# The first transfers of a recurrence-and-FFN kernel: x in four pieces, the gates' weights on another queue, one warming product less

## The chip, the cores and the metric

The kernel runs on one core of one Trainium2 chip. The metric is the device time of one execution in microseconds (us). The profile is one execution taken by the hardware profiler. Its engines are PE (TensorE: matrix products), PEld (TensorE's weight loads), DVE (VectorE), ACT (ScalarE), POOL (GpSimd) and SP (SyncE, which here issues nearly all transfers).

## The reference

The input x has 2 sequences of 4096 steps and 256 features. With sizes left out, the reference is

```python
u = x @ W_in + b_in                       # 64 states
g = sigmoid(x @ W_gate + b_gate)
h_t = tanh(h_{t-1} @ A + u_t @ Bm)         # along the 4096 steps
y_t = h_t @ C.T + u_t @ D.T
y_t = g_t * y_t + (1 - g_t) * x_t
x1  = layernorm(x + (y @ W_out + b_out + x))
ffn = gelu(x1 @ bin(w1).T + b1) @ bin(w2).T + b2   # bin(w) = mean|w| of a row times sign(w)
out = layernorm(x1 + ffn)
```

## The kernel before, in words

The recurrence is cut into segments: each sequence is split into 64 segments of 64 steps, so that one step handles 2 x 64 = 128 columns at once. The segments start from zero states 48 steps (`WARM`) ahead, and the kernel later checks that this warm-up was long enough. The steps are grouped into 16 chunks of 4 steps, with 512 columns each. One chunk's x in transposed form is a tile `xt` of 128 partitions x 2 x 512 numbers (512 KB); the middle index `k` is the half of the 256 features that lies on the partitions. The first chunk used is `FIRST` = 4, since the warm-up begins there; then come 5, 6 and so on.

The order of instructions on every engine is written out by hand, and each engine works its list in order. At the start TensorE's list is:

1. `idle_products`: products of a tile of ones with itself, which need no transfer (line 154).
2. `u_of_chunks(FIRST)`: u of chunk 4 (line 131). For each half `k` of the features there is one product for the first 256 columns (called LOW, written to the lower partitions of the result) and one for the other 256 (TOP). They need `wab` (W_in, A and Bm in one tile) and the tile `xt` of chunk 4. DVE and ACT add the bias and write u to `st` (lines 144 and 142).
3. `parts`: pieces of the gates' product of chunk 4 (line 313), which need `w_gate`, with a step of the recurrence (line 157; its tanh on ACT, line 158) put between each two.
4. `u_of_chunks(5, 6)`: u of chunks 5 and 6 together (line 131), where chunk 5 is LOW and chunk 6 is TOP. They need both tiles.
5. Further pieces of gates and steps, and u of the chunks 7 and 8, and so on. After the warm-up of the recurrence the later stages (mixing, projection, norms, the two layers of the FFN) are woven into the same list.

Each product of float32 numbers appears in the profile as two MATMUL passes.

The transfers at the start are issued by two engines, each with a queue of its own:

- ACT: `wab` (96 KB, line 109), `bias_c` (5.5 KB, line 111). After them comes its table load (line 120).
- SP: chunk 4 in two transfers of 256 KB, one for each `k` (line 104), `w_gate` (256 KB, line 112), then chunks 5, 6, 7, 8, 9, 10 and 11 whole (line 104), `cd`, `w_out`, and two rows of biases (lines 181 to 184).

A framework that builds the program gives each transfer one of eight completion semaphores in turn, and a transfer waits until the one that had the semaphore before it has landed. `x_tiles` has eight buffers (`XTB`), so later chunks also wait until a tile has been used.

Of the kernel before, what the change touches and what calls it, by code (L numbers as in the profile page):

```python
# [18 lines left out]
KD = DM // P  # L19
# [4 lines left out]
N = 512  # L24
# [13 lines left out]
def gated_recurrence_then_binary_ffn(  # L38
# [16 lines left out]
    nc = tc.nc  # L55
# [21 lines left out]
    w_gate = cp.tile([P, KD, DM], FP, name="w_gate")  # L77
# [20 lines left out]
    x_tiles = {}  # L98

    def load_xT(c, pieces=1):  # L100
        x_tiles[c] = xp.tile([P, KD, N], FP, tag="xt", name=f"xt{c}", bufs=XTB)
        for k in range(pieces):
            cut = slice(k * KD // pieces, (k + 1) * KD // pieces)
            nc.sync.dma_start(out=x_tiles[c][:, cut, :], in_=xT[c][:, cut, :])

    FIRST = (L - WARM) // SPC
    nc.gpsimd.memset(ones, 1.0)
    nc.gpsimd.memset(ab[:, S:], 0.0)
    nc.scalar.dma_start(out=wab[:, : KD * S + S], in_=W_in_AB)
    load_xT(FIRST, KD)  # L110
    nc.scalar.dma_start(out=bias_c, in_=biases)
    nc.sync.dma_start(out=w_gate, in_=W_gate)

    nc.gpsimd.memset(h_of[:, L - WARM, :, :], 0.0)
    nc.gpsimd.memset(h_of[:, 0, :, 0:1], 0.0)
# [8 lines left out]
    def u_of_chunks(*chunks):  # L124

        n = N * len(chunks) // 2
        parts = [(chunks[0], 0), (chunks[1], 0) if len(chunks) == 2 else (chunks[0], 1)]
        ps = p_1.tile([P, N], FP, tag="h", name=f"ps_u{chunks[0]}")
        for k in range(KD):
            for (c, i), r in zip(parts, (LOW, TOP)):  # L130
                nc.tensor.matmul(  # L131
                    ps[r, :n],
                    w_in[k],
                    x_tiles[c][:, k, bass.ts(i, n)],
                    start=k == 0,
                    stop=k == KD - 1,
                    skip_group_check=True,
                )
        for (c, i), r in zip(parts, (LOW, TOP)):
            to = u_of[:, bass.ds(c * SPC + i * n // W, n // W)].rearrange("p j b k -> p (j b k)")  # L140
            if r is TOP and c == FIRST:
                nc.scalar.activation(to, ps[r, :n], AF.Identity, bias=bin_c[r, :])
            else:
                nc.vector.tensor_scalar(to, ps[r, :n], bin_c[r, :], None, ALU.add)
        have_u.update(chunks)
        yield
# [4 lines left out]
    def idle_products(n):  # L151

        for _ in range(n):
            nc.tensor.matmul(p_h, ones, ones, start=True, stop=True)
# [174 lines left out]
    class Chunk:  # L329
# [10 lines left out]
        def load_gate_x(self):  # L340
            load_xT(self.c)
# [322 lines left out]
    def emit(what, pieces, pace=5600):  # L664
        nonlocal since
        for _ in pieces:
            since += COST.get(what, 0)
            if since >= pace:
                since = min(since - pace, pace // 2)
                if ready():  # L670
                    next_steps()
# [25 lines left out]
    with tc.manual_schedule(engines={ET.PE, ET.Activation, ET.DVE, ET.Pool, ET.SP}):  # L697
        waiting = []
        for c in range(FIRST + 1, FIRST + 6):
            load_xT(c)  # L700
        idle_products(7)
        emit("u", u_of_chunks(FIRST), 1 << 30)
        since = 0
        pairs = [(5, 6), (7, 8), (9, 10), (11, 12), (13, 14), (), (1, 2)]
# [224 lines left out]
```

## Time and profile before

| | before |
|---|---|
| median of 3 runs | 437.67 us (437.33 to 437.82) |
| time of the profiled execution | 437.67 us |
| its span, first to last instruction | 435.9 us |
| PE busy | 425.5 us, 98% of the span |
| DVE, ACT, POOL busy | 332.4, 286.0, 155.8 us |
| DMA moved | 51.34 MB, mean 118 GB/s |
| DMA in the first 5 of 40 slices | 297, 300, 282, 261, 269 GB/s |

All instants below are in us from the first instruction of the span. A profile line of a group gives line, engine, operation and tiles. In a timeline, the bracket at the end tells how long the engine was idle before the group and what ended it. "Busy" of PE means that a product was in its pipeline, not that it ran at its peak.

### The profile page before, as it was taken

To read this page: it belongs to the slowest core of one execution; us is meant where nothing else is said; L and a number is where in the kernel's file an instruction comes from. 1 tells how busy PE (TensorE), PEld (TensorE's weight loads), DVE (VectorE), ACT (ScalarE), POOL (GpSimd) and SP (SyncE) were. 2 spreads that over 40 slices of the span, in tenths; PEclk is the share of its full clock that TensorE was granted. 3 is DMA by queue.
4 is the path that set the end of the run, shared out by engine and by line. 5 is a ranking of instruction groups with operands and counts; after the bars stand their busy time and mean duration, and the time that the engine had idled before them with its cause. 6 is when DMAs were issued, how large, how long until landed. Compare 5 with 4: busy or idle time off the path is not lost.

```text
span 435.9 us, 6818 instructions
## 1 busy us (share of the span) xinstructions
PE 425.5 (98%) x2402; PEld 344.3 (79%) x2402; DVE 332.4 (76%) x569; ACT 286.0 (66%) x480; POOL 155.8 (36%) x176
## 2 busy tenths in 40 slices
PE   8999999999999999999999999999999999999992
PEld 5665767788888879797979797978888888888982
DVE  0245937895979798888888897979797979797674
ACT  2443452486587776767677776777767585849881
POOL 1000050474143435253525443444343444533413
PEclk9999999999999999999999999999999999999997
DMA  8877713400251615152426242534233232311102
GB/s 297 300 282 261 269 36 128 163 2 0 44 174 44 217 46 178 38 186 80 144 66 192 76 144 69 166 102 124 91 107 109 58 111 60 111 36 50 48 2 102
DMA packets 31479, 51.34 MB, mean 118 GB/s; under 512 B 5328, under 2 KB 19664, under 8 KB 31440
## 3 DMA queue, kind: packets, MB, share of 16 engines
q1 hardware_dynamic: 30864, 50.48, 36.4%
q8 instruction: 21, 0.34, 0.3%
q10 hardware_dynamic: 576, 0.37, 0.3%
q14 instruction: 18, 0.15, 0.1%
HBM read 31.43 MB, written 8.39 MB: 91 GB/s over the span
## 4 chain that ended last, share of the span: by engine, by line
PE 89%; DVE 5%; ACT 2%; DMA 1%; issue 1%; POOL 1%; SPq 0%; POOLq 0%; DVEq 0%
PE ps_h L486 25%; PE ps_o L528 25%; PE ps_g L313 12%; PE ps_z L399 11%; PE ps_y L374 6%; PE ps_s L157 6%; PE ps_u L131 3%; DMA xt<-in_xT 1%; DVE hlo L512 1%; ACT xn L278 1%; POOL rs_b L265 1%; PE ps_t L430 1%; DVE bs_b L255 1%; DVE d L381 1%; ACT h L496 1%
## 5 line engine op out<-in xcount | busy, mean ns | idle before, releaser
L528 PE MATMUL ps_o<-sg,hhi 128*128 128x256 f32 x496 | 121.4, 286 | 0.0
L528 PE MATMUL ps_o<-sg,hlo 128*128 128x256 f32 x496 | 117.9, 279 | 0.1
L496 ACT ACTIVATE h<-ps_h,bias_c,al 128x512 f32<-128x512 f32 x128 | 95.5, 771 | 16.8 <-PE ps_h L486 13.0
L528 PEld LDWEIGHTS ps_o<-sg,hhi 128*128 128x128 f32 x496 | 93.5, 189 | 1.1 <-DVE o L544 0.3
L528 PEld LDWEIGHTS ps_o<-sg,hlo 128*128 128x128 f32 x496 | 93.5, 188 | 1.1 <-DVE hlo L512 0.3
L486 PE MATMUL ps_h<-xhi,sg 128*128 128x512 f32 x256 | 92.9, 444 | 0.3 <-ACT h L496 0.3
L359 POOL TENSOR_TENSOR xn<-xn,bo_r 128x256 f32<-128x256 f32 x64 | 54.7, 888 | 88.6 <-DMA xn<-in_x 78.4
L512 DVE TENSOR_TENSOR hlo<-h,hhi 128x1024 fp32r<-128x1024 f32 (+1 forms) x65 | 79.5, 1240 | 5.0 <-ACT hhi L505 5.0
L486 PE MATMUL ps_h<-xlo,sg 128*128 128x512 f32 x256 | 80.1, 394 | 0.2
L265 POOL TENSOR_TENSOR rs_b<-rs_b,neg_half 128x4 f32<-128x4 f32 (+1 forms) x17 | 28.1, 1655 | 115.1 <-DVE rs_b L264 105.0
L505 ACT CAST hhi<-h 128x1024 fp32r<-128x1024 f32 (+1 forms) x65 | 67.4, 1039 | 2.0
L313 PE MATMUL ps_g<-xt,w_gate 128*128 128x384 f32 (+3 forms) x208 | 66.2, 430 | 0.1
L486 PEld LDWEIGHTS ps_h<-xhi,sg 128*128 128x128 f32 x256 | 46.5, 189 | 18.9 <-issue 11.7
L158 ACT ACTIVATE st<-ps_s 64x128 f32<-64x128 f32 x112 | 30.0, 268 | 45.7 <-PE ps_s L157 45.3
L486 PEld LDWEIGHTS ps_h<-xlo,sg 128*128 128x128 f32 x256 | 48.0, 188 | 11.9 <-DVE xlo L440 0.7
L157 PEld LDWEIGHTS ps_s<-st,wab 128*128 128x128 f32 x224 | 38.5, 189 | 21.6 <-ACT st L158 9.7
L359 POOL TENSOR_TENSOR xn<-xn,b_r 128x256 f32<-128x256 f32 x64 | 52.9, 855 | 1.1 <-PE ps_t L430 1.1
L399 PE MATMUL ps_z<-w_out,tg 128*128 128x256 f32 x224 | 50.6, 379 | 0.0
L399 PEld LDWEIGHTS ps_z<-w_out,tg 128*128 128x128 f32 x224 | 41.4, 190 | 5.1
L157 PE MATMUL ps_s<-st,wab 128*128 128x128 f32 x224 | 43.8, 277 | 0.1
L278 ACT ACTIVATE xn<-xn,nm_a,rs_a 128x256 f32<-128x256 f32 x60 | 31.2, 591 | 14.4 <-DVE nm_a L270 14.3
L265 POOL TENSOR_TENSOR rs_a<-rs_a,neg_half 128x4 f32<-128x4 f32 x16 | 17.2, 1072 | 65.0 <-DVE rs_a L264 63.0
(79 smaller groups left out, 481.5 us busy)
## 6 DMA issues: line engine op xcount, KB each, us to landing
xt<-in_xT SPq DMA_DIRECT2D x35, 512.0 KB, 4.4
xn<-in_x SPq DMA_DIRECT2D x16, 512.0 KB, 3.4
out_y<-xn SPq DMA_DIRECT2D x15, 512.0 KB, 2.6
xlo<-xb SPq DMA_DIRECT2D x208, 32.0 KB, 1.9
hu<-st SPq DMA_DIRECT2D x32, 128.0 KB, 2.3
w1t<-in_w1T SPq DMA_DIRECT2D x2, 512.0 KB, 4.9
w1n<-in_w SPq DMA_DIRECT2D x2, 512.0 KB, 6.1
w2t<-in_w2T SPq DMA_DIRECT2D x2, 512.0 KB, 5.2
```

The lines of the kernel that those rows point to most:

```text
L157: nc.tensor.matmul(p_h, ab, st[:, j].rearrange("p b k -> p (b k)"), start=True, stop=True)
L158: nc.scalar.activation(h_of[:, j + 1].rearrange("p b k -> p (b k)"), p_h[TOP, :], AF.Tanh)
L265: nc.gpsimd.tensor_tensor(rs, rs, neg_half[:, cut], ALU.pow)
L278: nc.scalar.activation(r, r, AF.Identity, bias=self.sh[:, i : i + 1], scale=rs)
L313: nc.tensor.matmul(ps[:, cut], w_gate[:, k, bass.ts(m, P)], xt_[:, k, cut], start=k == 0 and i == 0, stop=k == KD - 1, skip_group_check=True,)
L359: nc.gpsimd.tensor_tensor(r[:, i, :], r[:, i, :], row, ALU.add)
L399: nc.tensor.matmul(self.ps_z[:, i, :], self.y[:, k, bass.ts(i, P)], w_out[:, k, :], start=k == 0, stop=k == KD - 1,)
L486: nc.tensor.matmul(ps, sg1[:, k, bass.ts(j, P)], part[:, k, :], start=n == 0, stop=n == 2 * KD - 1,)
L496: nc.scalar.activation(to, ps.rearrange("p (a i c) -> p a i c", a=P // 32, c=32) if self.far else ps, AF.Gelu, bias=b1_c[:, j : j + 1], sc ...
L505: nc.scalar.copy(hi[:, part, :], h[:, part, :])
L512: nc.vector.tensor_sub(lo[:, i, :], h[:, i, :], hi[:, i, :].bitcast(FP))
L528: nc.tensor.matmul(ps[:, i, :], part[:, j % 2, bass.ts(tb, P)], sg2[:, j, :], start=j == 0 and part is self.h[j // 2][0] and first, stop=j ...
```

## The change

`load_xT` with `pieces=2` now cuts a chunk by half `k` and by half of the columns, so that the first chunk comes in four transfers of 128 KB, in the order in which its four products take them. A piece is 256 numbers, 1 KB, on each partition; before it was 512 numbers, 2 KB. `w_gate` is issued by ACT, between `wab` and `bias_c`, instead of by SP behind the first chunk. `idle_products` makes 6 products instead of 7. Nothing else in any engine's list changes its place; the semaphores of all later transfers move on by two.

```diff
     def load_xT(c, pieces=1):
         x_tiles[c] = xp.tile([P, KD, N], FP, tag="xt", name=f"xt{c}", bufs=XTB)
-        for k in range(pieces):
-            cut = slice(k * KD // pieces, (k + 1) * KD // pieces)
-            nc.sync.dma_start(out=x_tiles[c][:, cut, :], in_=xT[c][:, cut, :])
+        if pieces == 1:
+            nc.sync.dma_start(out=x_tiles[c], in_=xT[c])
+            return
+        for k in range(KD):
+            for i in range(pieces):
+                cut = bass.ts(i, N // pieces)
+                nc.sync.dma_start(out=x_tiles[c][:, k, cut], in_=xT[c][:, k, cut])
 
...
     nc.scalar.dma_start(out=wab[:, : KD * S + S], in_=W_in_AB)
-    load_xT(FIRST, KD)
+    load_xT(FIRST, 2)
+    nc.scalar.dma_start(out=w_gate, in_=W_gate)
     nc.scalar.dma_start(out=bias_c, in_=biases)
-    nc.sync.dma_start(out=w_gate, in_=W_gate)
...
-        idle_products(7)
+        idle_products(6)
         emit("u", u_of_chunks(FIRST), 1 << 30)
```

## The prediction

> **What bounds the kernel now.** I read the page first: shares, then the chain that ended last.
>
> ```profile
> PE 425.5 (98%) x2402; PEld 344.3 (79%) x2402; DVE 332.4 (76%) x569; ACT 286.0 (66%) x480; POOL 155.8 (36%) x176
> ...
> PE 89%; DVE 5%; ACT 2%; DMA 1%; issue 1%; POOL 1%; SPq 0%; POOLq 0%; DVEq 0%
> ```
>
> TensorE is busy nearly throughout and carries 89% of the chain. So a microsecond won or lost ahead of its unbroken stretch moves the end by about a microsecond, and one inside cover moves nothing. The edits lie in the first 9 us; which wait ends last there? The chain in order of time says it (start, duration, what):
>
> ```profile
> 2.14 0.43 SPq L104
> 2.57 0.04 issue
> 2.62 6.29 DMA xt<-in_xT
> 8.90 0.04 issue
> 8.94 1.93 PE ps_u L131 x6
> 10.87 0.42 PE ps_s L157 x2
> 11.29 0.66 PE ps_g L313 x4
> 11.95 0.22 PE ps_s L157 x2
> ```
>
> SP's issues run one behind the other, and the one begun at 2.62 lands at 8.90: it is the third tile, chunk 6 (the fifth entry on SP: two halves of chunk 4, `w_gate`, chunk 5, chunk 6). From 8.94 TensorE never stops: the windows 9 to 20, 20 to 40 and 40 to 60 us are 11.00, 20.00 and 20.00 us busy. **The landing of chunk 6 sets the time**, not the first x. TensorE's timeline shows how far ahead it was:
>
> ```profile
> 7.65 1.07 PE L131 MATMUL ps_u<-xt,wab 128*64 128x512 f32 x2
> 8.94 1.93 PE L131 MATMUL ps_u<-xt,wab 128*64 128x512 f32 x6 [0.22 <-DMA xt<-in_xT]
> ...
> 16.46 1.94 PE L131 MATMUL ps_u<-xt,wab 128*64 128x512 f32 x8
> ```
>
> Two of the eight passes for chunks 5 and 6 ran at 7.65 and the other six from 8.94. The next pair's eight take 1.94, no longer than those six, since the two halves run side by side. So the early two bought nothing: TensorE may reach this place as late as 8.94, **1.29 us later than it does**, at no cost.
>
> The waits of TensorE's weight loads up to 9.5 us (total, times, longest) are small before that:
>
> ```profile
> PEld ps_u L131 <- DMA xt<-in_xT: 1.6, 3, 1.1
> ...
> PEld ps_g L313 <- DMA w_gate<-in_W_gate: 0.6, 1, 0.6
> ...
> PEld ps_u L131 <- DMA wab<-in_W_in_AB: 0.3, 1, 0.3
> ```
>
> Only the 1.1 is chunk 6's. The rest, which the edits aim at, come before 7.65 and are inside the 1.29.
>
> Why does chunk 6 land at 8.90? The table by stretches (last columns: granted clock, DMA share, GB/s):
>
> ```profile
> 1.50:3.00 1.50, 1.50 (x9) 1.50 (x9) 0.00 (x0) 1.31 (x2) 0.29 (x1) 1.00 0.58 128
> 3.00:4.50 1.50, 1.50 (x9) 1.25 (x10) 0.00 (x0) 0.18 (x1) 0.00 (x0) 1.00 1.04 364
> 4.50:6.00 1.50, 1.38 (x9) 0.51 (x8) 0.64 (x2) 0.00 (x0) 0.00 (x0) 1.00 1.05 318
> 6.00:9.00 3.00, 2.75 (x14) 1.40 (x13) 0.02 (x1) 1.01 (x3) 0.00 (x0) 1.00 1.03 412
> ```
>
> From 3 us on the DMA engines are full. Landings, as issue plus "us to landing": first half of chunk 4 at 4.1, `wab` 4.3, second half 4.8, `bias_c` 5.0, `w_gate` 5.6, chunk 5 7.6, chunk 6 8.9, chunk 7 10.2. The last steps are 1.3 us for 512 KB, and 524 KB at 412 GB/s is 1.27: first in, first out at full rate. Chunk 6 is behind bytes, not behind its issue.
>
> **What the Trainium skill says.** "DMA: Bandwidth & Descriptors", section "Queues, rings and completion order": SP and ACT each own one row of rings on the same 16 engines, each ring consumed in order, the rows taken in turn by the packet. The trace agrees with order within SP's row (landings above). The same page, "Issuing engines are not separate DMA queues": a second issuing engine saves only issue time, here 0.43 us an issue. So `w_gate` on ACT's row shares the same rate. The same page, "Why small descriptors are slow (HBM only)": about 3 cycles for each packet beside one for each 32 bytes; 35 cycles for 1 KB against 67 for 2 KB is 4.5% more, an estimate. The trace's packet records have 84 ns for most 2 KB packets and 46 for most 1 KB ones, 9.5%; I take those. "TensorE: Matmul & The Clock Gate", Part 1: the clock doubles after some 3.4 us of sustained work. Here the warming passes begin at 1.01 and take 0.21 us each, against 0.11 for the same 128 columns at 11.95; the change comes at about 4.3.
>
> **The change, part by part.**
>
> *Four transfers for two.* SP issues four of 0.43 and loses `w_gate`'s: the pieces go at 0.76, 1.21, 1.67 and 2.14, chunk 5 at 2.62 instead of 2.14. Chunk 5's data wait for the ring anyway (5.5 us to landing, of which 1.3 is its own), so 0.48 is hidden; uncovered it would cost 0.48. The pieces' rows are 1 KB: 512 packets of 46 ns instead of 256 of 84, over 16 engines: 1.47 against 1.34, **+0.13 us** ahead of chunk 6, not hidden (0.06 by the skill's price).
>
> *Semaphores.* In the instruction list each DMA takes one of eight completion semaphores in turn, so the ninth waits for the first. Before, the first eight end with chunk 7, and chunk 8 waits for `wab`; SP's own waits show it:
>
> ```profile
> SPq L104 <- DMA wab<-in_W_in_AB: 0.8, 1, 0.8
> ```
>
> Now there are two more before, so **chunk 6 waits for `wab`**: issued at about 4.3 instead of 2.62. Queued behind it on SP are chunks 7 to 11, `cd`, `w_out`, the two rows; each waits for a DMA eight places ahead, long landed. Cover: first packets move 1.0 us after an issue (0.76 to 1.78), so chunk 6 is ready at about 5.3, while chunk 5 keeps the ring until about 7.1 (landing 7.6, some 0.5 after the last data by the packet records). 1.8 us of cover; cost 0. Chunks 7 and 8 aren't needed before 16.46.
>
> *`w_gate` on ACT.* Same bytes ahead of chunk 6; cost 0. It now shares with x, so it lands somewhat earlier than 5.6 and the last piece of x about when `w_gate` did, 5.5, instead of 4.8. The last products of chunk 4 take about 0.5: the gates begin at about 6.1 instead of 5.61, chunks 5 and 6 are reached at 8.15 instead of 7.65. Covered by the 1.29. ACT issues one more: `bias_c` goes at 1.65 and lands at 5.2 to 5.5, the table load ends at 3.4; ACT is first needed at 6.06, DVE's conversion moves by at most the same 0.5, and only the first steps wait for it, inside the same cover.
>
> *One product less.* Two passes, 0.43: TensorE is free at 3.94, but `wab` lands at 4.3. Gain 0. If the clock changes later: below, B.
>
> Sum: 0.13 and something for smaller packets in the slow opening, taken as **+0.15 us**. The profiled execution took 437.67 us (435.9 span, 1.8 around it), which is also the median: 437.8.
>
> The unknown is the opening. Against 412 GB/s the stretch 4.5 to 6 lacks 0.14 MB, or 0.34 us, and 1.5 to 3 lacks 0.43 MB, or 1.0 us. The trace gives no cause, and other packet sizes and rows may shift either. I take no change, and -0.35 to +0.5 as the likely bounds.
>
> **The rivals.**
>
> *A, likeliest:* as above, 437.8, own range 437.3 to 438.3. Chance 0.62.
>
> *B, slower: the clock.* With twelve passes TensorE idles from 3.94 to about 4.2, just where the clock rose. If it rises 3.4 us later, at 7.7, chunk 4 is done at 6.5, and of the 2.04 us of full-speed work up to chunks 5 and 6, 0.6 is done by 7.7: TensorE arrives at 9.1, +0.2. It decides from a rise later than about 7.5. A second miss, to 11.1, gives 10.4 for the arrival and about 12.5 for the end of those products instead of 10.7: +1.8, **439.5**. For it: fewer passes and new small waits for four pieces. Against: the busy share of the 3.3 us falls only to some 90%. Chance 0.08, mostly the dear end.
>
> *C, faster: a better opening.* Two rows with work from 1.2 us on fill the 0.34 or part of the 1.0. TensorE's arrival at 8.15, a little earlier when the pieces also land earlier, limits it to some -0.8 to -1.2. Typical **437.1**. Against: `wab` and x already shared the engines from both rows. Chance 0.16.
>
> *D, slower: chunk 6 issued too late.* If `wab` lands later than about 6, the ring runs dry and every further us costs one; or chunk 6's first packets, now fresh, have a slow start like the stretch at 4.5 (+0.34), with the first pieces' too (+0.5 more): **438.5**. Against: 96 KB at the head of its row. Chance 0.14.
>
> **How the numbers follow.** Prediction 437.8. A measurement of this kernel can tell about 0.2%, 0.88 us, from no change. A is inside it. C passes it in some 0.10 of its 0.16, B and D in some 0.18 of their 0.22, and 0.02 is put on each side for causes not thought of, taken from A: faster 0.12, same 0.68, slower 0.20. The range 436.9 to 438.8 takes in A, most of C and the nearer part of D; left out are the ends of C, D and B's second miss.
>
> **What would show it.** Right: in the new trace chunk 6's issue near 4.3, its landing at 8.8 to 9.3 with TensorE's wait for it still the longest at the start, then no gap; twelve warming passes; chunk 5's landing 1.3 before chunk 6's; gates at about 6. Wrong: a landing outside that, TensorE arriving after chunk 6 has landed, passes of 0.21 us for 128 columns after 7.7, or a DMA gap before chunk 6.

## The result, and the profile after

| | before | after |
|---|---|---|
| median, 22 runs of each | 437.97 us (437.15 to 438.61) | 438.62 us (438.13 to 440.56) |
| ratio | | 1.0016, 95% interval 1.0009 to 1.0023 |
| profiled execution | 437.67 us, span 435.9 us | 438.86 us, span 437.1 us |

The kernel became slower by 0.65 us. The interval leaves out no change, and its middle, 0.16%, is below the 0.2% that the prediction called the least to be told from no change. The predicted median was 437.8 and the predicted range ended at 438.8.

The page's shares first, then its shares of the chain that ended last:

```profile
PE 426.2 (98%) x2400; PEld 344.2 (79%) x2400; DVE 332.1 (76%) x569; ACT 285.8 (65%) x480; POOL 154.6 (35%) x176
...
PE 89%; DVE 2%; SPq 2%; ACT 2%; DMA 2%; issue 1%; POOLq 0%; POOL 0%; DVEq 0%; ACTq 0%
```

Two TensorE passes fewer; still busy nearly throughout and still 89% of the chain. The difference must be at the start. The chain there, in order of time (start, duration, what):

```profile
2.14 5.03 DMA xt<-in_xT
7.17 0.04 issue
7.21 0.65 PE ps_u L135 x2
7.86 0.84 PE ps_g L317 x2
8.70 0.29 PE ps_s L161 x2
8.99 0.66 PE ps_g L317 x4
9.65 0.22 PE ps_s L161 x2
9.87 1.87 PE ps_u L135 x8
11.74 0.42 PE ps_s L161 x2
```

The transfer that releases TensorE is no longer chunk 6 but the fourth piece of chunk 4: issued at 2.14, landed at 7.17. From there TensorE works without a gap into the eight passes for chunks 5 and 6. They end at 11.74; before, they ended at 10.87. That is **+0.87 us**. Product by product, the distance between the two traces stays there up to 240 us and grows in a few steps to the +1.19 of these two executions. (Before's execution lay 0.30 below its median, after's 0.24 above its own, so the medians differ by less.)

TensorE's timeline of the same stretch (start, duration; in brackets the idle time before a group and what ended it):

```profile
1.00 2.93 PE L158 MATMUL ps_s<-ones 128*128 128x128 f32 x12 [1.00 <-POOL ones L111]
3.87 2.48 PE L135 MATMUL ps_u<-xt,wab 128*64 128x256 f32 x6
7.21 0.65 PE L135 MATMUL ps_u<-xt,wab 128*64 128x256 f32 x2 [0.87 <-DMA xt<-in_xT]
...
9.80 1.94 PE L135 MATMUL ps_u<-xt,wab 128*64 128x512 f32 x8
```

Twelve warming passes, six of the eight passes for chunk 4, then a wait for the last piece. The bracket counts time with no product in the pipeline; the waits of the weight loads (total, times, longest) are longer:

```profile
PEld ps_u L135 <- DMA xt<-in_xT: 2.5, 3, 1.7
```

Before, this row had 1.6, 3 times, longest 1.1, and its 1.1 was chunk 6's. Now its 1.7 is the last piece's, and chunk 6 has no wait at all: it landed at 9.73, just ahead of TensorE's arrival at 9.80. Both came about as late, so curing either alone would have gained next to nothing.

What the DMA engines did (the last two columns are the DMA engines' busy share and GB/s), after:

```profile
3.00:4.50 1.50, 1.50 (x7) 0.93 (x5) 0.00 (x0) 0.65 (x2) 0.00 (x0) 1.00 1.03 336
4.50:6.00 1.50, 1.50 (x6) 0.58 (x4) 0.17 (x1) 0.00 (x0) 0.00 (x0) 1.00 1.01 304
6.00:7.50 1.50, 0.63 (x3) 0.19 (x2) 0.00 (x0) 0.00 (x0) 0.00 (x0) 1.00 0.81 262
7.50:9.00 1.50, 1.50 (x8) 0.79 (x7) 0.49 (x1) 0.47 (x1) 0.00 (x0) 1.00 0.98 393
3.00:9.00 6.00, 5.13 (x19) 2.49 (x18) 0.66 (x2) 1.11 (x3) 0.00 (x0) 1.00 0.96 324
```

The kernel before, over the two stretches that matter:

```profile
6.00:7.50 1.50, 1.50 (x10) 1.15 (x8) 0.02 (x1) 0.74 (x2) 0.00 (x0) 1.00 1.01 404
...
3.00:9.00 6.00, 5.62 (x29) 3.16 (x29) 0.66 (x2) 1.19 (x4) 0.00 (x0) 1.00 1.04 377
```

Over the same 6 us, 324 GB/s instead of 377 is 0.32 MB less; ahead of 3 us the change had moved 0.05 MB more. The 0.27 MB that are left are 0.65 us at the 412 GB/s of full flow. Chunk 6 landed 0.83 later. So most of its lateness goes with bytes not moved, and most of those are missing between 6 and 7.5, where the engines' busy share itself fell to 0.81 although chunks 5 and 6 had been issued at 2.61 and 3.71 and waited for nothing.

A transfer's landing is the slowest of its shares on the 16 DMA engines. The Trainium skill says so ("DMA: Bandwidth & Descriptors", section "Why a DMA increments its semaphore by 16 and not by 1"), and the trace has 16 completion steps for each transfer. The last piece's steps came from 5.12 on; fifteen of them were there by 6.25 and the last came at 7.17. The packet records between 6 and 7.5 show single packets that took up to 1.5 us more than usual: they are packets of 4 KB, as chunks 5 and 6 have them, usually 159 ns each, and the worst took 1.69 us. Before, the worst in that stretch was 0.15 over its usual time (1.0 in the stretch ahead of it).

### The profile page after: what moved, and what is told of

It reads as the page before. It is cut to its first block, busy times and chain, and to the rows that moved or that the text cites. A ratio compares the mean times of both kernels' runs of the same rounds, so it can differ in the third digit from the quotient of the medians.

```text
span 437.1 us, 6816 instructions
## 1 busy us (share of the span) xinstructions
PE 426.2 (98%) x2400; PEld 344.2 (79%) x2400; DVE 332.1 (76%) x569; ACT 285.8 (65%) x480; POOL 154.6 (35%) x176
## 4 chain that ended last, share of the span: by engine, by line
PE 89%; DVE 2%; SPq 2%; ACT 2%; DMA 2%; issue 1%; POOLq 0%; POOL 0%; DVEq 0%; ACTq 0%
PE ps_h L490 25%; PE ps_o L532 25%; PE ps_g L317 12%; PE ps_z L403 11%; PE ps_y L378 6%; PE ps_s L161 6%; PE ps_u L135 3%; SPq L459 2%; DMA xt<-in_xT 1%; ACT xn L282 1%; PE ps_t L434 1%; ACT h L500 1%; DMA xlo<-xb 0%; PE ps_p L532 0%; DVE bs_a L259 0%
## 5 line engine op out<-in xcount | busy, mean ns | idle before, releaser
L363 POOL TENSOR_TENSOR xn<-xn,bo_r 128x256 f32<-128x256 f32 x64 | 53.5, 870 | 90.7 <-DMA xn<-in_x 82.6
```

The source lines that it names most:

```text
L363: nc.gpsimd.tensor_tensor(r[:, i, :], r[:, i, :], row, ALU.add)
```

## The experiments

Times are set against runs of the kernel before on the same chip. "Landed" and "arrived" (TensorE's first pass for chunks 5 and 6) are of the one profiled execution. The prediction had put the cost of the pieces at +0.13 to +0.15 us and that of every other edit at nothing. The first four kernels do one part each.

**Pieces alone.** The change's `load_xT` and call; `w_gate` stays on SP, with seven warming products.

```diff
-    load_xT(FIRST, KD)
+    load_xT(FIRST, 2)
```

> The kernel before with the four pieces alone (w_gate stays on SP, seven warming products). Theory P (the pieces: 1 KB packets and one more slow packet each make the opening of the DMA engines slower, and the slowest engine sets chunk 6's landing): +0.4 to +0.8 us against before, chunk 6 landing at 9.3 to 9.9 instead of 8.9. Theory S (the turn of the eight semaphores: chunk 6 is issued only when wab has landed): the same here, since the pieces bring that turn with them. Theory G (w_gate on ACT's queue takes the rate from x): within 0.2. Theory W (the missing warming product): within 0.2.

Measured: 438.70 against 437.88, ratio 1.0020 (1.0013 to 1.0027), +0.8 us. Its chain, in order of time:

```profile
0.75 2.82 DMA wab<-in_W_in_AB
3.57 0.01 issue
3.59 7.15 DMA xt<-in_xT
10.73 0.04 issue
10.78 1.93 PE ps_u L135 x6
```

And its flow:

```profile
3.00:4.50 1.50, 1.50 (x9) 1.27 (x9) 0.17 (x1) 0.17 (x1) 0.00 (x0) 1.00 0.88 229
4.50:6.00 1.50, 1.50 (x7) 0.83 (x6) 0.00 (x0) 0.00 (x0) 0.00 (x0) 1.00 0.96 266
...
3.00:9.00 6.00, 5.77 (x25) 3.48 (x23) 0.66 (x2) 1.11 (x4) 0.00 (x0) 1.00 0.94 303
```

The cut of the first x alone gives the whole loss. The chain runs through chunk 6's wait for `wab`, which invites the reading that the semaphore's turn makes chunk 6 late. But SP was busy with its issue of chunk 5 until 3.52, so the wait itself is under 0.1 us, and the bytes are missing already between 3 and 6 us, before chunk 6's turn on the engines. The cost of the semaphore is tested below.

The traced execution is the slowest of the 19 (439.35), so its landing of chunk 6 is later than in most of them. One stretch of it shows another possible cause:

```profile
3.50:4.00 0.50, 0.50 (x5) 0.50 (x3) 0.00 (x0) 0.00 (x0) 0.00 (x0) 1.00 0.57 191
```

SP began a piece about every 0.47 us. 128 KB in that time is some 280 GB/s (an estimate from the issue times), less than the 412 that the engines moved at full flow, and here they were busy for 0.57 of the time while the first packet of `w_gate`, issued at 2.62, came only at 4.11. So part of this kernel's loss may be that the issues came too slowly. In the whole change that stretch shows a share of 1.04; its hole lies between 6 and 7.5, behind the pieces, when two whole chunks had long been issued, and slow issues don't explain that one. No kernel tests them alone.

**`w_gate` on ACT alone.**

```diff
+    nc.scalar.dma_start(out=w_gate, in_=W_gate)
     nc.scalar.dma_start(out=bias_c, in_=biases)
-    nc.sync.dma_start(out=w_gate, in_=W_gate)
```

> The kernel before with w_gate alone moved to ACT between wab and the biases. Chunk 6 is still among the first eight transfers and waits for no semaphore. Theory G: +0.4 to +0.8 us, second half of chunk 4 landing at 5.5 or later instead of 4.8. Theories P, S and W: within 0.2 us of before, chunk 6 landing at 8.6 to 9.1.

Measured: 438.06, ratio 1.0004 (0.9998 to 1.0011): no change. The timeline of TensorE shows two things that cancel in the traced execution:

```profile
5.79 0.91 PE L313 MATMUL ps_g<-xt,w_gate 128*128 128x384 f32 x2
7.80 0.46 PE L157 MATMUL ps_s<-st,wab 128*128 128x128 f32 x2 [1.10 <-DVE st L144]
...
9.07 1.94 PE L131 MATMUL ps_u<-xt,wab 128*64 128x512 f32 x8
```

Chunk 6 landed at 8.35, 0.55 earlier than before. But `bias_c` stands behind `w_gate` in ACT's queue and landed only at 6.94, so the first step waited and TensorE arrived at 9.07. Whether the move made chunk 6 early isn't shown: over kernels with the first x in two transfers its landing varies from 8.35 to 9.76.

**Six warming products alone.**

```diff
-        idle_products(7)
+        idle_products(6)
```

> The kernel before with six warming products alone. Theory W: the clock rises later and the time is up by 0.3 us or more, with TensorE reaching chunks 5 and 6 after 8.9. Theories P, S and G: within 0.2 us; the clock may rise later, but TensorE still waits for chunk 6.

Measured: 437.78, ratio 1.0001 (0.9992 to 1.0009): no change. By the trace's clock records TensorE's clock rose at 3.91 here, with fewer products, and at 4.31 before.

**The semaphores' turn alone.** Two extra transfers of 5.5 KB on ACT's queue move the turn by two, as the change does.

```diff
     nc.scalar.dma_start(out=wab[:, : KD * S + S], in_=W_in_AB)
+    for i in range(2):
+        spare = cp.tile([P, 1 + KD + KH], FP, name=f"spare{i}")
+        nc.scalar.dma_start(out=spare, in_=biases)
```

> The kernel before with two more transfers of the biases (5.5 KB each, into tiles that nothing reads) issued by ACT behind bias_c, which moves the turn of the semaphores on by two, as the change does, and leaves the x of chunk 4 in two transfers. Theory S: chunk 6 is issued when wab has landed, near 4.3, and lands at 9.3 to 9.9: +0.4 to +0.8 us. Theories P, G and W: it is ready before the engines have done chunk 5, and lands at 8.7 to 9.2: within 0.2 us.

Measured: 440.66, ratio 1.0074 (1.0060 to 1.0087), +2.8 us, but not at the start. Chunk 6, issued at 4.24 when `wab` had landed, landed at 8.40, and up to 100 us TensorE was 0.5 ahead of before. From 100 us on it lost about 0.06 at a time in the products of the later stages. The costliest groups of this kernel (busy us, mean ns of one):

```profile
L531 PE MATMUL ps_o<-sg,hhi 128*128 128x256 f32 x496 | 123.4, 287 | 0.0
L531 PE MATMUL ps_o<-sg,hlo 128*128 128x256 f32 x496 | 120.0, 279 | 0.0
```

The same groups of the kernel before:

```profile
L528 PE MATMUL ps_o<-sg,hhi 128*128 128x256 f32 x496 | 121.4, 286 | 0.0
L528 PE MATMUL ps_o<-sg,hlo 128*128 128x256 f32 x496 | 117.9, 279 | 0.1
```

The same 992 passes, 2.0 and 2.1 us more of busy time (the two groups overlap, so this is no sum), with not one instruction of theirs changed. What the new tiles change is the addresses of the tiles behind them, so the loss here says nothing on the semaphores. The next kernel has no new tiles; the tiles alone come further below.

**The semaphores' turn, in place.** The two transfers now write into `al2_r`, a row that is filled later.

```diff
+    for i in range(2):
+        nc.scalar.dma_start(out=al2_r[:, bass.ds(16 * i, 1 + KD + KH)], in_=biases)
```

> The kernel before with the two additional transfers of the biases again, this time into a tile that exists (al2_r, written over later), so that no address in SBUF moves. Chunk 6 waits for wab as after the change. Theory S (turn of the semaphores): +0.4 to +0.8 us. Theory P (the pieces) as well as theory A (the loss of the earlier run with two tiny transfers came from the moved addresses of later tiles, which its trace shows as a drift from 100 us on, while chunk 6 landed early): within 0.2 us, chunk 6 landing at 8.3 to 9.2, and no drift.

Measured: 437.80 against 437.85, ratio 1.0001 (0.9993 to 1.0009): no change, though chunk 6 was issued at 4.29, when `wab` had landed, as its chain shows:

```profile
0.75 3.52 DMA wab<-in_W_in_AB
4.27 0.02 issue
4.29 5.47 DMA xt<-in_xT
9.76 0.04 issue
```

The median has no cost, and the interval ends at 0.09%, or 0.4 us, below the change's 0.65. So the semaphores' turn alone does not make the loss. It may not be free in every execution: in the traced one chunk 6 was late (9.76), and 5 of the 13 runs took 438.46 to 438.73 as it did (438.63), against one of 39 of the kernel before. TensorE's timeline of this kernel, whose list is that of the kernel before, tells one more thing:

```profile
4.32 1.97 PE L133 MATMUL ps_u<-xt,wab 128*64 128x256 f32 x8
...
8.62 3.11 PE L133 MATMUL ps_u<-xt,wab 128*64 128x512 f32 x8
```

Before, the first of these lines was:

```profile
4.32 1.16 PE L131 MATMUL ps_u<-xt,wab 128*64 128x256 f32 x8
```

The eight passes for chunk 4 took 1.97 instead of 1.16. Here the clock rose at 7.18 by its records, and TensorE arrived at 8.62 instead of 7.65. The cover of 1.29 us that the prediction read from the profile was the cover of one execution with an early rise.

**Pieces with rows of 2 KB.** Four transfers of 128 KB again, cut by partitions instead of columns, so that the packets stay at 2 KB; all else as in the pieces alone, against which the diff is.

```diff
-                cut = bass.ts(i, N // pieces)
-                nc.sync.dma_start(out=x_tiles[c][:, k, cut], in_=xT[c][:, k, cut])
+                rows = bass.ts(i, P // pieces)
+                nc.sync.dma_start(out=x_tiles[c][rows, k, :], in_=xT[c][rows, k, :])
```

> The kernel before with chunk 4 in four transfers of 128 KB cut by partitions (64 partitions of 2 KB rows) instead of by columns; w_gate stays on SP, seven warming products. Theory P1 (the smaller packets cost): within 0.3 us of before. Theory P2 (the number of transfers in SP's ring costs, whatever their rows, or the later issue of w_gate and chunk 5 behind them): +0.5 to +1.0 us, as with the four pieces alone, with chunk 5 landing late and its sixteen shares spread over 2 us.

Measured: 439.05, ratio 1.0030 (1.0022 to 1.0038), +1.2 us. So there is a loss without any packets of 1 KB in x. The kernel isn't clean, though: SP's issues of these took about 0.59 each instead of 0.43, so chunk 5 went out at 3.94 instead of 2.14, and a piece of 128 KB every 0.64 us is some 205 GB/s (an estimate as above). How much of the loss is due to this is not known, and the two sizes of packet can't be compared by it. Chunk 6 landed at 10.61.

**The change with three transfers.** The first half `k` in two pieces, the second whole; all else as in the change. Now chunk 6 is eighth and waits for no semaphore, and chunks 5 and 6 are issued at 2.14 and 2.61, as before. The diff is against the change.

```diff
-            for i in range(pieces):
-                cut = bass.ts(i, N // pieces)
+            n = pieces if k == 0 else 1
+            for i in range(n):
+                cut = bass.ts(i, N // n)
```

> The changed kernel with three pieces: the first half of the features in two transfers of 128 KB, the second in one of 256 KB. Chunk 6 is the eighth transfer again and waits for no semaphore. Theory S: the loss of 0.65 us goes, within 0.2 of before. Theory P: about half of it stays, +0.2 to +0.5 us.

Measured: 438.71 against 437.85, ratio 1.0027 (1.0016 to 1.0038): a loss as large as the change's, without its wait. The chain has chunk 6 issued at 2.61 and landing late all the same:

```profile
2.61 7.09 DMA xt<-in_xT
9.70 0.04 issue
```

Beside the other two edits, each of which cost nothing alone (both without a cut were not tried), one extra cut is enough. The loss needs neither the semaphores' wait nor a later issue of chunks 5 and 6. It is not half of the change's, as it would be if each cut cost the same.

**A third part first.** A kernel for the bound itself: one more piece of gates and one step are put ahead of chunks 5 and 6, so that TensorE works while chunk 6 is on its way. Transfers as before.

```diff
-            before = 2 if n == 0 else 1
+            before = 3 if n == 0 else 1
```

> The kernel before with three parts of chunk 4's gates (and a third step) ahead of the products of chunks 5 and 6 instead of two, 0.87 us of TensorE's work moved out of the stretch behind the wait into the wait. If chunk 6's landing is what ends last at the start, as the prediction says: 0.5 to 0.9 us faster than before. If TensorE was as late as the landing in most executions, or the steps then wait for DVE: within 0.2 us.

Measured: 437.40 against 437.85, ratio 0.9990 (0.9982 to 0.9998), **-0.45 us**. TensorE's timeline:

```profile
8.12 0.82 PE L313 MATMUL ps_g<-xt,w_gate 128*128 128x256 f32 x4
8.78 0.39 PE L157 MATMUL ps_s<-st,wab 128*128 128x128 f32 x2
9.10 1.94 PE L131 MATMUL ps_u<-xt,wab 128*64 128x512 f32 x8
```

Chunk 6 landed at 8.78 and TensorE arrived at 9.10, having done 0.88 us of work that before came after. The gain is a little below the 0.5 to 0.9 that was expected. This is the fastest of all kernels here, and it shows that the wait for chunk 6 was the bound. It was not joined with other edits.

**`w_gate` on ACT behind the biases.**

```diff
     nc.scalar.dma_start(out=bias_c, in_=biases)
-    nc.sync.dma_start(out=w_gate, in_=W_gate)
+    nc.scalar.dma_start(out=w_gate, in_=W_gate)
```

> The kernel before with w_gate issued by ACT, but behind bias_c, so that the biases aren't late as they were (6.9 us) with w_gate ahead of them. Chunk 5 leaves SP 0.47 us earlier. Theory P (only the splitting of the first x costs): within 0.2 us of before, or faster by up to 0.5 if chunk 6 lands early, as it did at 8.35 with w_gate ahead of the biases. Theory G (w_gate on a second queue costs by its traffic): +0.3 us or more.

Measured: 439.92 against 438.08, ratio 1.0039 (1.0026 to 1.0052), +1.8 us. `w_gate` landed at 7.86, as its packets took turns with chunk 5's. The windows (third column from the right: granted clock) show what followed:

```profile
5.50:8.00 2.50, 0.10 (x1) 0.10 (x1) 0.49 (x1) 0.47 (x1) 0.00 (x0) 0.96 1.02 406
8.00:11.40 3.40, 3.40 (x10) 2.54 (x10) 0.00 (x0) 0.27 (x1) 0.00 (x0) 0.53 1.03 420
11.40:14.00 2.60, 2.60 (x14) 1.14 (x13) 0.56 (x1) 0.43 (x2) 0.00 (x0) 1.00 1.01 399
```

TensorE stood idle for 2.4 us, lost half its clock from 7.81 to 11.23, and arrived at 11.45, when chunk 6 had been there since 8.94. This is the mechanism of rival B, in a kernel that leaves TensorE idle. The loss came by `w_gate`'s lateness and not by chunk 6's: that landed as before.

**The first x whole.** The opposite of the change: one transfer of 512 KB.

```diff
-    load_xT(FIRST, KD)
+    load_xT(FIRST)
```

> The kernel before with the x of chunk 4 in one transfer of 512 KB with rows of 4 KB instead of two. Theory P (each cut of the first x lengthens the slowest engine's delay, by about 0.4 us a cut): 0.2 to 0.5 us faster than before, chunk 6 landing at 8.3 to 8.8. Theory N (cutting in two costs nothing, only smaller pieces do): within 0.2 us; chunk 4's products then begin at 4.9 instead of 4.3, inside TensorE's cover.

Measured: 438.11 against 438.08, ratio 1.0003 (0.9990 to 1.0016). Its windows:

```profile
3.00:4.50 1.50, 1.36 (x7) 1.06 (x5) 0.00 (x0) 0.17 (x1) 0.00 (x0) 1.00 1.02 393
4.50:6.00 1.50, 0.95 (x6) 0.58 (x8) 0.17 (x1) 0.00 (x0) 0.00 (x0) 1.00 1.06 408
...
3.00:9.00 6.00, 5.31 (x20) 3.27 (x19) 0.66 (x2) 0.64 (x2) 0.00 (x0) 1.00 1.04 409
```

The flow is full from 3 us on, no packet after 3 us is over 0.18 us late, and chunk 6 landed at 8.09. But TensorE waited from 4.36 to 5.05, and in this execution (439.61 us) its clock rose only at 10.22, so it arrived at 10.47. The 14 runs fall into two groups of seven, 437.01 to 437.47 and 438.75 to 439.81; the traced one is of the slower. So the gain that the early landing promised is not in the median.

**Two unused tiles.** The tiles of the fourth experiment, 44 bytes on each partition, without their transfers.

```diff
+    for i in range(2):
+        cp.tile([P, 1 + KD + KH], FP, name=f"spare{i}")
```

> The kernel before with two tiles of 44 bytes a partition that nothing uses, allocated where the first run with two tiny transfers had its own; no transfer more. Theory A (its loss of 2.8 us came from the addresses of the later tiles, moved by 88 bytes): +2.5 to +3.5 us, growing evenly along the products with the signs of w1 and w2 from 100 us on. If the transfers caused it: within 0.3 us of before.

Measured: 441.38 against 438.08, ratio 1.0079 (1.0065 to 1.0094), +3.3 us. TensorE's list is that of the kernel before, product by product. What is left to make the loss is where the later tiles lie.

**The first x whole and nine warming products.** The two more products close the gap before chunk 4's.

```diff
-    load_xT(FIRST, KD)
+    load_xT(FIRST)
...
-        idle_products(7)
+        idle_products(9)
```

> The kernel before with the x of chunk 4 in one transfer and nine warming products instead of seven, so that TensorE is busy until that transfer has landed (nine end at 5.2, the first products began at 5.05). With the whole x chunk 6 landed at 8.09, but the idle time from 4.4 to 5.05 left the clock at half until 10.2 and TensorE came at 10.4. Theory C (chunk 6's landing and TensorE's arrival, which hangs on when the clock rises, are both near the bound): with the gap closed the clock rises by 7.3 at the latest, TensorE arrives at 8.3 to 9.3, and the time is 0.2 to 0.7 us below before. If the clock has nothing to do with it: as with the whole x alone, within 0.2 us of before.

Measured: 437.91 against 437.95, ratio 1.0001 (0.9991 to 1.0010). In the profiled execution it worked: chunk 6 landed at 8.17, TensorE arrived at 8.35 and was 0.59 ahead of before at 10 us; the execution took 437.48. The median shows no gain, and its runs spread from 436.94 to 439.08. Whether runs with a late clock eat the gain was not seen, since only one execution has a trace: inconclusive as to the time.

The kernels together, by the number of transfers that bring the first x (two kernels with moved addresses are left out):

| first x in | kernels | GB/s from 3 to 9 us | chunk 6 landed | cost |
|---|---|---|---|---|
| 1 transfer | whole; whole with nine products | 409, 411 | 8.09, 8.17 | 0, by two groups; 0 |
| 2 transfers | before; `w_gate` on ACT; six products; turn in place; third part; behind biases | 377, 382, 373, 370, 365, 392 | 8.90, 8.35, 9.16, 9.76, 8.78, 8.94 | 0 unless told above |
| 3 transfers | three pieces | 333 | 9.70 | +0.9 |
| 4 transfers | the change; pieces alone; 2 KB rows | 324, 303, 293 | 9.73, 10.73, 10.61 | +0.65, +0.8, +1.2 |

The order of the four rows holds for the flow without exception; the cost does not follow it, as three pieces cost no less than four. These are single executions, and those of the pieces alone and of the 2 KB rows are the slowest of 19 and the second slowest of 14. Two things besides the number of transfers differ: the one transfer also has packets of 4 KB instead of 2 KB, and in the pieces alone and the 2 KB rows SP's issues came more slowly than the engines move bytes. That the number alone sets the flow is not shown.

**What stays open** is why more cuts make the flow worse. The runs exclude the semaphores' turn and `w_gate`'s queue, each taken alone, and a later issue of chunks 5 and 6 as a necessary cause; small packets are not needed for a loss, but their share in it was not measured. In the profiled executions the latest single packet between 3 and 9 us was 1.4 to 1.8 us over its usual time in the kernels with three and four transfers, 0.6 to 1.2 with two (0.3 in the kernel with two tiny transfers in new tiles) and 0.14 to 0.18 with one. With three and four, the engines' busy share fell to 0.81 to 0.88 in some stretch of 1.5 us; in the others it did not go below 0.93. Whether the late packets make the others wait, or both have a third cause, was not tried.

## Why the prediction was right, and which term was mis-sized

- **The bound: right.** The start decides. A kernel with TensorE's list filled before chunk 6 gains 0.45; the change shifts the end of chunks 5 and 6 by +0.87 in the trace, and the rest of the kernel keeps the distance.
- **The sign and the size's class: right, but not by the account that was held likeliest.** A small loss below 0.2% was forecast, with a range that reached to 438.8. Rival A's own range, 437.3 to 438.3, was missed; 438.62 is in the range because that took in the nearer part of D. Of the signs that the prediction named for being wrong, three came: chunk 6 landed outside 8.8 to 9.3, TensorE arrived (9.80) after it had landed (9.73), and the DMA flow had a hole before it (share 0.81). Of those for being right, the unbroken stretch behind it, the twelve passes and the 1.3 us between chunks 5 and 6 came; the others did not. That the number came out near is in part luck.
- **The sum's term for the pieces: too small.** The step "I take no change" for the opening failed. The sum had +0.15; measured were +0.65, and +0.8 for the pieces alone. The +0.65 is the sum with the opening at its upper bound of +0.5; the +0.8, and the +0.87 in the trace, are beyond it. The +0.13 for smaller packets is a part of this at most. The opening was called the unknown with the right resource, but its bounds were read from what the trace before lacked (0.34 us), and only rival D put a price on what new pieces may add.
- **The last piece: wrong.** It was to land at about 5.5 and landed at 7.17, so TensorE arrived at 9.80 instead of 8.15, and the chain went through it.
- **Chunk 6's landing: wrong.** Predicted at 8.8 to 9.3, measured 9.73. Its issue at 3.71 instead of 4.3 is the same mechanism, `wab` having landed earlier (3.70). That wait is not what made the loss: the turn in place has it without a loss in the median, three pieces have the loss without it.
- **The cover of 1.29 us: overstated.** It held for the profiled execution. With the clock rising at 6.86 and 7.18, as in two other kernels with that TensorE list, TensorE arrives at 8.58 and 8.62, and the cover is about 0.3.
- **`w_gate` on ACT and one product less: right at nothing.** Alone, 1.0004 and 1.0001, both intervals holding 1. The bias landed at 5.39, inside the 5.2 to 5.5. With `w_gate` alone moved, the bias came at 6.94 and held TensorE up past chunk 6's landing in that trace; this was not foreseen.
- **Rival A against D.** Counted from before's median of 437.97 instead of 437.67, A's 437.8 becomes 438.1 and D's 438.5 becomes 438.8; the measured 438.62 lies between, nearer to D. Of D's two triggers the late issue of chunk 6 did not make the loss; its other, a slow start of the first pieces and of chunk 6, is nearest to what the trace shows.
- **Rival B (the clock): not what decided.** In the traced execution the clock rose at 6.54, earlier than the 7.5 from which B was to cost anything, and the pieces alone lose as much with all seven warming products. Its mechanism is real, as the kernel with `w_gate` behind the biases shows.
- **Rival C (a better opening): refuted for the cut.** In the traces the fuller opening came with the first x in one transfer, not four.

## What to carry to other kernels

Cutting a first transfer so that work can start sooner is worth something only if the work that starts sooner is the bound; here it was not, and with the cuts the later transfer that was the bound came later. Before cutting, set SP's time for one issue (about 0.43 us here, 0.6 for the pieces by partitions) against the time that the piece takes at full flow (0.32 us for 128 KB at 412 GB/s). Read a transfer's cost by the slowest of its 16 shares and by the flow over the whole opening, and give a cut an uncertainty as wide as the late packets that are already in the trace (1.0 us here). Where a wait at the start can't be shortened, put work ahead of it: moving one piece and one step gained 0.45 us (ratio 0.9990, 0.9982 to 0.9998).

## What the runs showed of the hardware that was not expected

- Two unused tiles of 44 bytes a partition cost 3.3 us, 0.8%, with every product of TensorE's list unchanged: the tiles behind them lie elsewhere. Any experiment that adds a tile has to be read with this in mind.
- The rise of TensorE's clock varied from 3.9 to 7.2 us between executions whose warming passes all began at 1.0, and was 10.2 in one with a gap of 0.7 us. The Trainium skill ("TensorE: Matmul & The Clock Gate", Part 1) has a window that runs freely and gives a spread of half a microsecond; the spread here is 3.3 us, and 2.9 between two kernels with the same TensorE list (4.31 and 7.18). In the kernel with `w_gate` behind the biases the clock records begin at 4.40, 7.81 and 11.23, steps of 3.4 us; the spread is about one such step. The window table's clock column shows 1.00 until the first record; only the lengths of the passes tell the half clock there.
- With 512 KB of x in one transfer the opening moved about 410 GB/s, in two 365 to 392, in three or four 293 to 333, each in single executions. Why is open.
